# Moving the context queries of three units to earlier places in a fused transformer block

## The chip, the cores and the metric

The kernel runs on one core of one Trainium2 chip. The core has TensorE (PE, matmuls; PEld are its weight loads), VectorE (DVE), ScalarE (ACT), GpSimd (POOL) and SyncE (SP), which here issues nearly all DMAs. The engines run side by side, each through its own list of instructions in a fixed order, and wait for each other on semaphores. The metric is the device time of one execution in microseconds: 1073.81 us is the median of three runs before the change (1072.66 to 1074.61). A profiled execution of the same program took 1075.05 us.

## The reference

One transformer block in fp32, for 2 batches of 1024 tokens of width 256, 16 heads of 64, and a context of 154 tokens of width 192:

```
h = layernorm(x, ln1);  x = attention(h, h,        sa_wq, sa_wk, sa_wv, sa_wo, sa_bo) + x
h = layernorm(x, ln2);  x = attention(h, cond_emb, ca_wq, ca_wk, ca_wv, ca_wo, ca_bo) + x
h = layernorm(x, ln3);  p = h @ ff_w1 + ff_b1;  a, gate = p[..., :DF], p[..., DF:]
out = (a * gelu(gate)) @ ff_w2 + ff_b2 + x

attention: q = xq @ wq; k = xkv @ wk; v = xkv @ wv     (16 heads of 64)
           softmax(q @ k.T / 8) @ v, heads joined, @ wo + bo
```

Everything must be computed for both batches. The self-attention has 1024 keys a head, the context attention 154.

## The kernel before, in words

**Units and slots.** A unit is a batch and a pair of heads: 2 x 8 = 16 units, in the order `units` (unit 0 is batch 0, pair 0; unit 8 is batch 1, pair 0). Self-attention goes through the units in 128 slots `p`, 8 for each unit; slots 120 to 127 belong to unit 15. Context attention follows with 48 slots `c`, 3 for each unit: slot `c` belongs to unit `c // 3`, and `n = c % 3` is its place in it. Then comes the feed-forward stage.

**The order is written out by hand.** All engines' instructions stand in the order in which the two loops record them (`manual_schedule`). There is no planner that reorders them. Each engine works its own list strictly in that order.

**A self-attention slot** (`self_first`, loop at L1324 ff.). TensorE computes scores of 128 rows against 1024 keys in two PSUM tiles (`s`, L526; a tile is two banks, and there are two tiles). VectorE takes the maxima (L712), ScalarE the exponentials (L537) and frees the tile. The halves of a row lie on different partitions, so SP exchanges their maxima and sums by four small DMAs (`exchange`, L547, tile `st`). `join` then works out the factors (GpSimd L555 to L568, ScalarE L561), VectorE takes reciprocals (L640), GpSimd scales the rows (L650), and VectorE transposes them (`turn_group`, L675), one to three slots after their scores. When a half unit's transposes are complete, `self_values` multiplies them by the values (`po`, L578), in two parts, at slots with `p % 4` of 3 and 0. The value products also read a copy of the values with the partition halves exchanged, which `move_values` (L453) makes by DMA in the sixth slot of a unit. The other slots have room for other TensorE work, which `run_work(n, n_side, ...)` takes from three queues: `work` first (projections; each names the number of PSUM banks that it takes, and `n` is reduced by it), then `side` (normalisation of a later stage), then with what is left of `n` `outs` (output projections, `py`, L500).

**The last unit.** `self_beside(15)` puts the context queries of unit 0 (`cross_queries`, `pq_ca`, L369) into `work`, and the values of the context for units 0 and 1 (`context_values`, `pv_ca`, L831) into `held`, which joins `work` at slot 124. Slots 125 and 126 have `n = 1`. Slot 126 also computes the context keys of the last two pairs (`context_keys`, `pk`, L790).

**A projection** of queries: `project_both` (L369) multiplies the normalised, transposed tokens `hT_ln` by one 128-column slice of `ca_wq`, in two PSUM banks, one for each half of the tokens. With `m=KB` the matmuls use 32 columns of the array each, and with `m=HR` 64 columns. ScalarE evacuates both banks (L384) into a tile `q`, from a pool with two buffers for each tag. Queries use the tag `QT`; the self-attention's keys use `KT`.

**PSUM.** `mm_tile` hands out two banks by turns, `sum_tile` two others, and the scores have four. Whoever gets a bank waits until its previous content has been read.

**Slices.** `load_weights` loads a slice of a weight in two DMAs on SP (L134). For `ca_wq` an even pair's slice goes to the buffer `wq`, an odd pair's to `wk`; each tag has one buffer, so a load waits until the queries of two units before have been computed. In context attention the slice of unit `ui + 2` is asked for in the second slot of unit `ui`.

**A context slot** (`cross_first`). Scores for three or two groups of 128 rows (`sc`, L871), maxima (L877), exponentials (L888), reciprocals (L896), scaling on GpSimd (L899), transposes two slots later (`cross_turn`, L915). Once a unit is complete, `cross_regroup` sorts the result by eight DMAs (`wf<-pT_ca`, L932), and `cross_weigh` multiplies by the values (`poc`, L951) in the second slot of a unit, two units later. `cross_values` does this in two parts: the first writes two `sum_tile` banks, the second two `mm_tile` banks. VectorE evacuates `poc` (L965).

**What runs beside the first context slots**: slot 0 the second part of the value products of half 30, slot 1 the queries of unit 1, slot 2 those of unit 2 (in `sum_tile` banks), slots 3 and 4 the value products of the last half, slot 5 two output projections of self-attention (`py_sa`; four are queued there), slot 6 the queries of unit 3 and, in slot 7, a third `py_sa`, the context values of units 2 and 3 (`pv_ca`), the fourth `py_sa` and the first `poc`. From slot 9 on, the first slot of each unit `ui` computes the queries of unit `ui + 1`. In slot 7, ScalarE evacuates `pv_ca` (L841) and VectorE adds `py_sa` to `x` (L507).

**SP's own order** around the end of self-attention: exchange of slot 126, two copies within `held_v` (L843) that belong to `context_values` and are popped from the queue `later`, the slice of unit 2, the exchange of slot 127, four copies of `ends` (L848), the slice of unit 3.

Of the kernel before, what the change touches and what calls it, by code (L numbers as in the profile page):

```python
# [8 lines left out]
F32 = mybir.dt.float32  # L9
# [4 lines left out]
P = 128  # L14
# [4 lines left out]
def tile_transformer_block(ctx: ExitStack, tc: tile.TileContext, a: dict, out: bass.AP):  # L19
# [4 lines left out]
    B, S, D = x.shape  # L24
# [11 lines left out]
    HR = P // 2  # L36
# [3 lines left out]
    KB = 32  # L40
# [20 lines left out]
    p2 = ctx.enter_context(tc.tile_pool(name="p2", bufs=2))  # L61
# [64 lines left out]
    def load_slice(name, c0, n, p):  # L126

        own = w[name][:, c0:c0 + n]
        if p != HR:
            return load_rows(wpool, name[3:], f"{name}_{c0}", own, p)  # L130
        tag = "wk" if name == "ca_wq" and c0 // P % 2 else name[3:]
        t = wpool.tile([P, NH, n], F32, tag=tag, name=f"{name}_{c0}")
        for r0 in range(0, P, HR):
            nc.sync.dma_start(out=t[r0:r0 + HR], in_=own.rearrange("(c p) f -> p c f", p=HR))  # L134
        return t
# [3 lines left out]
    def load_weights(kind, pr, what):  # L139
        if what != "v":  # L140
            wsl[kind, pr, what] = load_slice(f"{kind}_w{what}", pr * P, P, HR)
        elif pr % 2 == 0:
            wsl[kind, pr, what] = load_slice(
                f"{kind}_w{what}", pr * P, VC, HR if kind == "sa" else CC)
# [71 lines left out]
    hT, vs, qk, oT = {}, {}, {}, {}  # L216
# [239 lines left out]
    def costing(n, fn):  # L456

        fn.banks = n
        return fn
# [14 lines left out]
    def self_pieces(b, pr):  # L474


        def q():
            self_unit(b, pr)
            return self_queries(b, pr)

        def k():
            pk = two_banks(f"pk_sa{b}_{pr}")
            project_both(pk, wsl["sa", pr, "k"], hT["sa", b], KB)
            return lambda: take_both(qk["sa", b, pr][1], pk)

        return [costing(2, q), costing(2, k)]
# [104 lines left out]
    def run(piece):  # L591
        done = piece()
        if done is not None:
            (adds if getattr(done, "adds", False) else stores).append(done)
# [32 lines left out]
    units = [(b, pr) for b in range(B) for pr in range(NPAIR)]  # L627
    NU = len(units)
# [94 lines left out]
    held, kept = [], []  # L723

    def self_beside(ui):

        nxt = self_pieces(*units[ui + 1]) if ui + 1 < NU else cross_pieces(*units[0])
        if ui + 1 < NU:
            if ui % 2 == 0 and ui:
                work.append(value_piece(*units[ui], 1))  # L730
            work.extend(nxt)
            if ui == 0:
                work.append(unit_value_piece(*units[1], 0, GT))
            if ui % 2:
                work.append(value_piece(*units[ui + 1], 0))
        else:

            work.extend(nxt[:1])
            held.extend(nxt[1:])
        if ui >= HP:  # L740
            ob, og = divmod((ui - HP) // HP, NQ)
            t0 = (ui % HP) * 2
            out_pieces("sa", ob, og, out_order("sa")[t0:t0 + 2])
        if ui == 1:
            norm_beside("sa", 1)
        if ui in (4, 6):
            add_biases("sa", (ui - 4) // 2)
        if ui == NPAIR + 1:
            norm_beside("ca", 0)

    def load_ahead(p):

        ui, n = divmod(p, 2 * SH)
        for what in "qkv":
            at = {"q": SH - 1 + 2 * (ui == 0), "k": SH + 2, "v": 2 * SH - 1}[what]
            if n != at or ui + 2 >= NU and what == "k":
                continue
            if what == "v" and ui % 2:
                continue
            if ui + 2 < NU:  # L760
                load_weights("sa", units[ui + 2][1], what)
            elif ui + 2 == NU or what == "q":
                load_weights("ca", units[ui + 2 - NU][1], what)
        if p == SA - 2:
            load_weights("ca", units[2][1], "q")
        if p in (LAG + 1, 2 * SH - 1, SA - SH - 6):
            load_keys(2 * (1 + (LAG + 1, 2 * SH - 1, SA - SH - 6).index(p)), 2)

# [2 lines left out]
    CA = len(CG) * NU  # L771
    crossed, pTc = {}, {}

    def cross_queries(b, pr, m=HR, bank=mm_tile):
        q = qk["ca", b, pr] = p2.tile([P, S], F32, tag="QT", name=f"q_ca{b}_{pr}")
        pq = [bank(f"pq_ca{b}_{pr}_{r}") for r in range(2)]
        project_both(pq, wsl["ca", pr, "q"], hT["ca", b], m)
        return lambda: take_both(q, pq, scale)
# [485 lines left out]
    with tc.manual_schedule():  # L1264
# [59 lines left out]
        for p in range(SA):  # L1324
# [21 lines left out]
            ui, n = divmod(p, 2 * SH)  # L1346
# [6 lines left out]
            if hg == LAG:  # L1353
                f = (ui - NPAIR // 2 - 1) * EC
# [4 lines left out]
                if n == SH + LAG and ui in (0, 1, NU - 1):  # L1359

                    pr = {0: 2, 1: 4, NU - 1: 6}[ui]
# [3 lines left out]
        for c in range(CA):  # L1365
# [13 lines left out]
            ui, n = divmod(c, len(CG))  # L1379
            nxt = units[ui + 1] if ui + 1 < NU else None  # L1380
            if n == 0:
                cross_beside(ui)
            elif n == 1 and 1 <= ui < NU - 2:
                load_weights("ca", units[ui + 2][1], "q")
            elif n == 2 and nxt and ui:
                load_weights("ca", nxt[1], "v")
            flush(adds)
# [17 lines left out]
            if c == 0:  # L1405
                run(lambda: self_values(2 * NU - 2, 1))
            elif c == 1:
                run(lambda: cross_queries(*nxt))
            elif c == 2:
                run(lambda: cross_queries(*units[2], bank=sum_tile))  # L1410
            elif c == 3:
                run(lambda: self_values(2 * NU - 1, 0))
            elif c == 4:
                run(lambda: self_values(2 * NU - 1, 1))
            elif n == 0 and ui:
                if nxt:
                    run(lambda: cross_queries(*nxt))
                else:
                    run_work(2, 0)
                run_work(0, 1)  # L1420
            elif n == 1:

                spare["turned"] = True
                run_work(0, 1, sum_tile if outs else None)
                flush(stores)
                run_work(0, 0, n_sum=1)
                if ui % 2 == 0:
                    run(lambda: context_values(*units[ui]))
                run_work(1, 0)
                flush(adds)  # L1430
                flush(slow)
                flush(stores)
                cross_weigh(c)
            elif n == 2:
                run_work(0, ui != HP, sum_tile if ui == HP + 1 else None)
                if c == SH + 1:
                    run_work(2, 0)
                elif ui == HP:
                    wo["ca"] = const.tile([P, NPAIR, D], F32, tag="wo", name="ca_wo")
                    later[1:1] = [lambda i=i: nc.sync.dma_start(  # L1440
                        out=wo["ca"][:, i, :], in_=w["ca_wo"][i * P:(i + 1) * P, :])
                        for i in range(NPAIR)]
# [20 lines left out]
        for k in range(2 * FU):  # L1463
# [18 lines left out]
            while n_left > 0 and sums:  # L1482
                fn, n = sums.pop(0)
# [51 lines left out]
```

## Time and profile before

| | |
|---|---|
| median of three runs | 1073.81 us (1072.66 to 1074.61) |
| profiled execution | 1075.05 us, its span 1073.2 us |
| granted TensorE clock | 1.0 throughout |
| busy: PE, PEld, DVE, ACT, POOL | 1059.4, 716.2, 883.1, 646.9, 777.0 us |
| self-attention, from the start of the span to about | 697.6 us (first context scores `sc`) |
| context attention to about | 897 us (last `sc`) |
| feed-forward | the rest |

A row of a timeline has the start in us from the beginning of the span, the duration in us, the engine, the line, the operation, output and inputs, tile, shape and number of instructions that were merged in this row; in brackets the idle time of the engine before it and what ended it. Matmuls overlap in the pipeline, so a row's duration reaches beyond the next row's start; the time that a group takes is better read from start to start. One fp32 matmul stands as two records. A row of `SPq` is the time that SP spends issuing; the transfer lands later. A line number such as L369 is the line of a helper and shared by all callers, so the tile's name (`pq_ca`, `pq_sa`) tells which.

### The profile page before, as it was taken

Reading aid. Unit: us, or ns where it says so; the run is one execution under the profiler, and the core shown is the slowest. Engines: PE = TensorE matmul, PEld = TensorE weight load, DVE = VectorE, ACT = ScalarE, POOL = GpSimd, SP = SyncE. Lnnn points to the kernel's source line nnn. Section 1 sums busy time; section 2 is a strip of 40 time slices with the busy share of each in tenths; the row PEclk is TensorE's granted clock in tenths of the full one; section 3 lists DMA queues with packets and bytes.
Section 4 is the critical chain, followed back from the end, with each engine's and each line's share of the span. In section 5 each row is a group of like instructions: output and inputs, shape, how many; then the busy total and the mean of one; then the engine's idle time right before and its main releaser. Section 6 shows DMA issues by size and latency. Waiting matters only on the chain.

```text
span 1073.2 us, 48628 instructions
## 1 busy us (share of the span) xinstructions
PE 1059.4 (99%) x20196; PEld 716.2 (67%) x20196; DVE 883.1 (82%) x1321; ACT 646.9 (60%) x2096; POOL 777.0 (72%) x1652
## 2 busy tenths in 40 slices
PE   8999999999999999999999999999999999999998
PEld 6566777556556555555665665466766667788998
DVE  5789899998989989999999899968777887655554
ACT  5766677677666666676777666665566564342231
POOL 2677777778777777677777777776666876499884
PEclk9999999999999999999999999999999999999999
DMA  3132122121021121111111101125776545000000
GB/s 101 38 73 54 29 68 53 25 63 41 22 59 25 34 51 34 39 34 34 44 22 45 44 14 38 36 59 139 164 177 172 123 108 114 16 6 15 21 10 30
DMA packets 86045, 60.95 MB, mean 57 GB/s; under 512 B 32122, under 2 KB 74562, under 8 KB 85826
## 3 DMA queue, kind: packets, MB, share of 16 engines
q1 hardware_dynamic: 84450, 57.07, 22.1%
q8 instruction: 159, 2.61, 1.1%
q10 hardware_dynamic: 1376, 0.79, 0.2%
q14 instruction: 60, 0.49, 0.2%
HBM read 27.91 MB, written 2.10 MB: 28 GB/s over the span
## 4 chain that ended last, share of the span: by engine, by line
PE 74%; DMA 7%; SPq 6%; POOL 6%; DVE 2%; issue 2%; ACT 1%; POOLq 0%; DVEq 0%; ACTq 0%
PE s L526 14%; PE po L578 13%; DMA st<-st 7%; SPq L547 6%; PE py_ca L500 5%; PE py_sa L500 4%; PE poc L951 4%; PE pq_ca L369 4%; PE pq_sa L369 4%; PE pb L1072 4%; PE pk_sa L369 4%; PE pq L1217 3%; PE pv_sa L405 3%; POOL p L650 3%; PE sc L871 2%; PE pa L1072 2%
## 5 line engine op out<-in xcount | busy, mean ns | idle before, releaser
L650 POOL TENSOR_SCALAR p<-p,rd,ee 128x512 f32<-128x512 f32 x512 | 391.9, 771 | 80.0 <-DVE rd L640 79.6
L537 ACT ACTIVATE p<-s,st 128x512 f32<-128x512 f32 x512 | 345.5, 687 | 169.7 <-DVE st L712 164.5
L712 DVE TENSOR_REDUCE st<-s 128x2 f32<-128x1024 f32 x256 | 308.6, 1206 | 56.8 <-issue 17.3
L675 DVE STREAM_TRANSPOSE pT<-p 128x1024 f32<-128x1024 f32 x256 | 302.8, 1219 | 1.5 <-POOL p L650 1.2
L526 PE MATMUL s<-k_sa,q_sa 64*32 64x512 f32 x4096 | 257.8, 591 | 2.8 <-ACT p L537 2.0
L578 PE MATMUL po<-pT,held_v 64*32 64x256 f32 x8192 | 240.8, 376 | 0.7 <-DVE pT L675 0.6
L578 PEld LDWEIGHTS po<-pT,held_v 64*32 64x32 f32 x8192 | 182.5, 106 | 67.0 <-issue 26.0
L526 PEld LDWEIGHTS s<-k_sa,q_sa 64*32 64x32 f32 x4096 | 89.7, 106 | 93.1 <-issue 46.6
L888 ACT ACTIVATE p<-sc,neg 128x154 f32<-128x154 f32 x256 | 96.4, 405 | 78.9 <-DVE rden L896 75.0
L899 POOL TENSOR_SCALAR p<-p,rden 128x154 f32<-128x154 f32 x256 | 97.3, 406 | 51.8 <-DVE rden L896 51.5
L537 ACT ACTIVATION_READ_ACCUMULATOR p<-s,st 128x1 f32 x512 | 104.0, 203 | 0.0
L555 POOL TENSOR_TENSOR dd<-st 128x8 f32<-128x8 f32 x128 | 26.0, 203 | 82.4 <-DMA st<-st 80.6
L500 PE MATMUL py_sa<-sa_wo,o_sa 128*128 128x256 f32 x256 | 59.7, 386 | 1.0 <-ACT held_v L415 1.0
L500 PE MATMUL py_ca<-ca_wo,o_ca 128*128 128x256 f32 x256 | 60.2, 383 | 0.0
L877 DVE TENSOR_REDUCE neg<-sc 128x6 f32<-128x924 f32 (+1 forms) x48 | 47.8, 996 | 14.9 <-PE sc L871 14.9
L369 PE MATMUL pq_ca<-hT_ln,ca_wq 64*64 64x512 f32 (+1 forms) x544 | 59.1, 590 | 0.9 <-DMA ca_wq<-in_L_xattn_ca_wq_dram 0.8
L500 PEld LDWEIGHTS py_sa<-sa_wo,o_sa 128*128 128x128 f32 x256 | 47.3, 190 | 19.0 <-issue 5.2
L369 PE MATMUL pq_sa<-hT_ln,sa_wq 64*32 64x512 f32 (+1 forms) x976 | 57.8, 586 | 0.7 <-ACT held_v L415 0.7
L369 PE MATMUL pk_sa<-hT_ln,sa_wk 64*32 64x512 f32 x960 | 57.1, 590 | 0.2 <-ACT q_sa L384 0.2
L888 ACT ACTIVATION_READ_ACCUMULATOR p<-sc,neg 128x1 f32 x256 | 56.5, 221 | 0.0
L915 DVE STREAM_TRANSPOSE pT_ca<-p 128x480 f32<-128x480 f32 (+1 forms) x96 | 52.9, 587 | 0.9 <-POOL p L899 0.8
L405 PE MATMUL pv_sa<-sa_wv,hT_ln 64*32 64x256 f32 x1792 | 52.9, 376 | 0.0
(158 smaller groups left out, 1476.0 us busy)
## 6 DMA issues: line engine op xcount, KB each, us to landing
wf<-pT_ca SPq DMA_DIRECT2D x128, 128.0 KB, 2.4
st<-st SPq DMA_DIRECT2D x512, 1.0 KB, 2.0
held_v<-held_v SPq DMA_DIRECT2D x32, 256.0 KB, 4.0
sa_wq<-in_L_xattn_sa_wq_dram SPq DMA_DIRECT2D x32, 128.0 KB, 2.8
sa_wk<-in_L_xattn_sa_wk_dram SPq DMA_DIRECT2D x32, 128.0 KB, 3.6
sa_wv<-in_L_xattn_sa_wv_dram SPq DMA_DIRECT2D x16, 256.0 KB, 4.2
ca_wq<-in_L_xattn_ca_wq_dram SPq DMA_DIRECT2D x32, 128.0 KB, 3.1
wf<-in_L_xattn_ff_w_dram SPq DMA_DIRECT2D x12, 256.0 KB
```

What stands on the lines that cost most here:

```text
L369: nc.tensor.matmul(pq[r][f:f + m, at:at + n], lhsT=wt[own, c, f:f + m], rhs=h[own, c, t0:t0 + n], start=(c == 0), stop=(c == NH - 1), tile ...
L405: nc.tensor.matmul(pv[r][f:f + KB, e * VC:(e + 1) * VC], lhsT=h[half, c, t0:t0 + KB], rhs=wt[half, c, :], start=(c == 0), stop=(c == NH - ...
L500: nc.tensor.matmul(py[:, e * D:(e + 1) * D], lhsT=o[:, i, (t + e) * P:(t + e + 1) * P], rhs=wo[kind][:, g * HP + i, :], start=(i == 0), st ...
L526: nc.tensor.matmul(sc[a4 * KB:(a4 + 1) * KB, j, :], lhsT=q[r, c:c + KB], rhs=k[r, h * HB:(h + 1) * HB], start=True, stop=True, tile_positi ...
L537: nc.scalar.activation(pr[:, j, :], sc[:, j, :], AF.Exp, bias=st[:, 0, 0, i, j:j + 1], accum_out=st[:, 0, 1, i, j:j + 1],)
L578: nc.tensor.matmul(po[a2][d:d + KB, :QH // 2], lhsT=v[e][r, t, d:d + KB], rhs=pT[r, d // DH * NK + n, :], start=(t == 0 and e == 0), stop= ...
L650: nc.gpsimd.tensor_scalar(pr[:, j, :], pr[:, j, :], own["rd"][:, c:c + 1], own["ee"][:, 0, c:c + 1], op0=ALU.mult, op1=ALU.mult,)
L675: nc.vector.transpose(halves[h][:, :, c:c + KB], slots[p]["p"][i].rearrange("p j (n k) -> p (j n) k", k=KB))
L712: nc.vector.tensor_reduce(st[:, 0, 0, i, :], sc[i], AX.X, ALU.max, negate=True)
L888: nc.scalar.activation(pr_[:, j, i, :T], sc[:, j, i * T:(i + 1) * T], AF.Exp, bias=neg[:, j, i:i + 1], accum_out=den[:, j, i:i + 1],)
L899: nc.gpsimd.tensor_scalar(pr_[:, j, i, :T], pr_[:, j, i, :T], rden[:, j, i:i + 1], 1.0, op0=ALU.mult, op1=ALU.mult,)
L1072: nc.tensor.matmul(into[:, :BT], lhsT=lhs, rhs=wh[pair][i], start=first, stop=True, skip_group_check=True)
```

## The change

Five edits, one of them the consequence of another:

- The queries of unit 1 leave context slot 1 and join `held`, ahead of the context values. They take two banks, with `m=KB` and the tag `KT`. By the rules of `run_work` they run in slot 125, and the context values, which ran there, in slot 126. The two copies within `held_v` that follow the context values move behind them, into context slot 0, on SP after the exchange of slot 127.
- The queries of units 2 and 3 run in context slots 1 and 2, unit 2 with the tag `QT` in `mm_tile` banks, unit 3 with the tag `KT` in `sum_tile` banks.
- Slot 6 has no queries any more, so it takes two from `outs` (`run_work(2, 0)`): the third and fourth `py_sa` move there from slot 7, and their additions on VectorE to the beginning of slot 7, ahead of its maxima.
- The slice of unit 3 is asked for in slot 126, behind that of unit 2, and so ahead of the exchange of slot 127.
- In context attention the slice of unit `ui + 3`, no longer `ui + 2`, is asked for in the second slot of unit `ui`. It goes into the buffer that the queries of unit `ui + 1`, computed one slot earlier (for unit 2 three slots earlier), have read.

From slot 9 on all engines have the same instructions in the same order as before, but for the slices. TensorE has 16 matmuls more in all, since the queries of unit 1 now use 32 columns each.

```diff
@@ self_beside, for the last unit
             work.extend(nxt[:1])
+            held.append(costing(2, lambda: cross_queries(*units[1], KB, tag="KT")))
             held.extend(nxt[1:])
@@ load_ahead
         if p == SA - 2:
-            load_weights("ca", units[2][1], "q")
+            for u in (2, 3):
+                load_weights("ca", units[u][1], "q")
@@ cross_queries
-    def cross_queries(b, pr, m=HR, bank=mm_tile):
-        q = qk["ca", b, pr] = p2.tile([P, S], F32, tag="QT", name=f"q_ca{b}_{pr}")
+    def cross_queries(b, pr, m=HR, bank=mm_tile, tag="QT"):
+        q = qk["ca", b, pr] = p2.tile([P, S], F32, tag=tag, name=f"q_ca{b}_{pr}")
@@ the loop over context slots
-            elif n == 1 and 1 <= ui < NU - 2:
-                load_weights("ca", units[ui + 2][1], "q")
+            elif n == 1 and 1 <= ui < NU - 3:
+                load_weights("ca", units[ui + 3][1], "q")
...
             elif c == 1:
-                run(lambda: cross_queries(*nxt))
+                run(lambda: cross_queries(*units[2]))
             elif c == 2:
-                run(lambda: cross_queries(*units[2], bank=sum_tile))
+                run(lambda: cross_queries(*units[3], bank=sum_tile, tag="KT"))
...
             elif n == 0 and ui:
-                if nxt:
+                if nxt and ui > 2:
                     run(lambda: cross_queries(*nxt))
                 else:
                     run_work(2, 0)
```

## The prediction

> **What bounds the kernel now.** I read the page first, then the busy time by stretches, then the timelines of TensorE and of the engines and queues that release it. The page:
>
> ```profile
> span 1073.2 us, 48628 instructions
> ## 1 busy us (share of the span) xinstructions
> PE 1059.4 (99%) x20196; PEld 716.2 (67%) x20196; DVE 883.1 (82%) x1321; ACT 646.9 (60%) x2096; POOL 777.0 (72%) x1652
> ```
>
> TensorE has 1073.2 - 1059.4 = 13.8 us without a matmul in the whole span. A change that only reorders work can win little more than what part of these holes it fills. The stretches where the change works (columns: PE, PEld, DVE, ACT, POOL busy):
>
> ```profile
> 680.00:690.00 10.00, 8.74 (x161) 4.25 (x139) 9.94 (x13) 6.76 (x23) 7.40 (x17) 1.00 0.12 29
> 690.00:700.00 10.00, 9.38 (x243) 5.13 (x249) 8.92 (x11) 6.26 (x21) 7.48 (x18) 1.00 0.38 95
> 740.00:750.00 10.00, 9.05 (x142) 5.26 (x138) 9.86 (x27) 7.48 (x36) 9.50 (x28) 1.00 0.61 157
> ```
>
> TensorE lacks 1.26 and 0.62 us in the last self-attention slots (125 to 127) and 0.95 us in the third and fourth unit of context attention; VectorE is nearly full in the first and the third. Their TensorE rows (start, duration, what, idle before it):
>
> ```profile
> 683.85 1.13 PE L831 MATMUL pv_ca<-ca_wv,ctxT 96*128 96x256 f32 x4
> 686.00 1.09 PE L526 MATMUL s<-k_sa,q_sa 64*32 64x512 f32 x16 [1.02 <-ACT p L537]
> 687.33 1.09 PE L526 MATMUL s<-k_sa,q_sa 64*32 64x512 f32 x16 [0.24 <-ACT p L537]
> 688.36 2.42 PE L790 MATMUL pk<-ctxT,ca_wk 96*128 96x320 f32 x8
> 691.09 1.09 PE L526 MATMUL s<-k_sa,q_sa 64*32 64x512 f32 x16 [0.31 <-ACT p L537]
> 692.42 1.09 PE L526 MATMUL s<-k_sa,q_sa 64*32 64x512 f32 x16 [0.24 <-ACT p L537]
> 693.31 4.36 PE L578 MATMUL po<-pT,held_v 64*32 64x256 f32 x128
> ```
>
> Slot 125 has only `pv_ca` beside its scores, and the scores of 126 and 127 wait in four halves (1.02, 0.24, 0.31, 0.24) for a PSUM bank that ScalarE's exponentials hold. That is the room for the moved queries. The softmax tail meets TensorE again at context slot 3:
>
> ```profile
> 711.96 3.69 PE L578 MATMUL po<-pT,held_v 64*32 64x256 f32 x128 [0.61 <-DVE pT L675]
> ```
>
> Here 0.61 us is lost to VectorE's last transposes: up to 0.61 us of lateness of TensorE costs nothing; lateness of the softmax costs in full.
>
> **The change part by part.**
>
> *Queries of unit 1 in slot 125.* Sixteen wide matmuls leave context slot 1; thirty-two narrow ones (32 columns, twice the weight loads) enter. The first unit's queries have that form already:
>
> ```profile
> 662.69 3.64 PE L369 MATMUL pq_ca<-hT_ln,ca_wq 64*32 64x512 f32 x64
> ```
>
> 3.64 us against 3.67 for the wide form (725.31, below): the form costs nothing. Start to start I take 3.43 (725.31 to 728.74). Their slice is asked for only in slot 123:
>
> ```profile
> 680.09 1.39 SPq L134 DMA_DIRECT2D ca_wq<-in_L_xattn_ca_wq_dram  x2
> ```
>
> ```profile
> ca_wq<-in_L_xattn_ca_wq_dram SPq DMA_DIRECT2D x6, 128.0 KB, 3.9
> ```
>
> The second half goes out at about 680.8 and, at 3.9 us to land, is there at 684.7; the queries run to 684.7 + 3.43 = 688.1. Then the scores of 126 (half of 64 such records, 1.72), `pv_ca` now in this slot (0.86, from 731.53 to 732.39 below) and `pk` (2.42): the scores of 127 begin at 693.1 (before 691.09), the value products at 694.8 (before 693.31). But before, these had to wait anyway:
>
> ```profile
> 694.44 2.75 PEld L578 LDWEIGHTS po<-pT,held_v 64*32 64x32 f32 x104 [0.55 <-DMA held_v<-held_v]
> ```
>
> After 24 loads they stood until 694.44 for the moved half of the values, so they ended at 693.31 + 4.36 = 697.7. Now, without that wait, 694.8 + 3.43 and the pipeline's 0.2 give 698.4: 0.7 late, 0.1 more than the 0.61 at slot 3 covers.
>
> *The softmax beside it.* VectorE took the first half of 126 late already:
>
> ```profile
> 688.40 1.15 DVE L712 TENSOR_REDUCE st<-s 128x2 f32<-128x1024 f32 x1
> ```
>
> It will be there at 688.1 + 1.09 = 689.2, 0.8 later. The evacuation of the new queries comes ahead of 126's exponentials on ScalarE, but while these still wait for the maxima: nothing. What counts is the exchange of slot 127 on SP:
>
> ```profile
> 696.74 0.21 ACT L537 ACTIVATION_READ_ACCUMULATOR p<-s,st 128x1 f32 x1
> ```
>
> ```profile
> 695.89 1.23 SPq L843 DMA_DIRECT2D held_v<-held_v  x2
> 697.16 1.35 SPq L134 DMA_DIRECT2D ca_wq<-in_L_xattn_ca_wq_dram  x2
> 698.67 3.20 SPq L547 DMA_DIRECT2D st<-st  x4
> ```
>
> The exponentials of 127 end at 696.95, the exchange leaves at 698.67: the queue came last, with 1.72 to spare. The change swaps the two copies of `held_v` for the two loads of unit 3's slice (1.23 against 1.35, +0.1); that load waits for the queries of slot 125, done at 688.1, so for nothing. The copies follow behind the exchange, some 30 us ahead of their reader (734.21). If 126's exchange, at the head of this queue, slips by its 0.8, so does 127's. Tail in all: between -0.6 (the hole at slot 3 closes, where the transposes come sooner by chance) and +0.9. I take +0.2, because the nearest row, 698.67, stands behind a queue.
>
> The larger load ahead of the exchange is weighed against a rule: the Trainium skill, "DMA: Bandwidth & Descriptors", section "Queues, rings and completion order", says each DMA engine consumes its ring in order, so a small transfer behind a slice waits for it. No row here separates that wait. With the 435 GB/s of the page's section "Specifications" the 128 KB more are an estimated 0.3 us, and the sum would come out 0.3 higher.
>
> *Units 2 and 3 in context slots 1 and 2.* Same form, banks and slots as units 1 and 2 had: 0. Nobody waits for them; their first scores are slots 6 and 9. The second buffer tag is free, as the keys it held were last read in slots 119 and 127.
>
> *Slots 6 and 7.* The stretch before:
>
> ```profile
> 725.31 3.67 PE L369 MATMUL pq_ca<-hT_ln,ca_wq 64*64 64x512 f32 x32
> 728.74 1.03 PE L871 MATMUL sc<-kT,q_ca 64*64 64x154 f32 x24
> 729.70 1.99 PE L500 MATMUL py_sa<-sa_wo,o_sa 128*128 128x256 f32 x8
> 731.53 1.03 PE L831 MATMUL pv_ca<-ca_wv,ctxT 96*128 96x256 f32 x4
> 732.39 1.89 PE L500 MATMUL py_sa<-sa_wo,o_sa 128*128 128x256 f32 x8
> 734.21 1.09 PE L951 MATMUL poc<-wf,held_v 64*64 64x256 f32 x16
> ...
> 736.85 1.49 PE L871 MATMUL sc<-kT,q_ca 64*64 64x154 f32 x40
> ```
>
> The two `py_sa` (1.83 + 1.82 = 3.65) move up into slot 6 in place of the queries (3.43): slot 7's scores start 0.22 late, at 728.96. `pv_ca` follows at 729.9, `poc` could begin at 731.0 and end at 733.6, 3.2 before 736.85. It will not. `poc` has two parts of half its 2.64 us each, and the second writes the two rotating matmul banks. Before, `py_sa` ran between `pv_ca` and `poc` and hid `pv_ca`'s evacuation. Now that cover is gone, and ScalarE does it behind slot 7's exponentials:
>
> ```profile
> 731.07 0.39 ACT L888 ACTIVATE p<-sc,neg 128x154 f32<-128x154 f32 x1 [0.96 <-DVE rden L896]
> ```
>
> ```profile
> 733.27 0.76 ACT L841 COPY held_v<-pv_ca 64x256 f32<-64x256 f32 x2
> ```
>
> ```profile
> 729.83 1.12 DVE L877 TENSOR_REDUCE neg<-sc 128x6 f32<-128x924 f32 x1 [0.89 <-PE sc L871]
> ```
>
> ```profile
> 732.29 0.63 DVE L507 TENSOR_TENSOR x<-py_sa,x 128x512 f32<-128x512 f32 x1
> ```
>
> Worse, the two additions of `py_sa` now stand ahead of slot 7's maximum: the second waits for its matmuls (728.96) and 0.63 more, so the maximum starts near 730.2 instead of 729.83. The copies then end at 733.27 + 0.76 + 0.4 = 734.4; the rest of the second part (1.32 less a sixth, and 0.1 to the release) ends at 735.6. The next scores start 736.85 - 735.6 = 1.2 us sooner, not 3.2. Bounds: 0 and 3.2. From there VectorE is full (9.86 of 10), all its work hangs on that point and moves with it.
>
> *Slices asked sooner.* One hole remains:
>
> ```profile
> 747.95 1.04 PE L369 MATMUL pq_ca<-hT_ln,ca_wq 64*64 64x512 f32 x2
> 749.83 3.23 PE L369 MATMUL pq_ca<-hT_ln,ca_wq 64*64 64x512 f32 x27 [0.85 <-DMA ca_wq<-in_L_xattn_ca_wq_dram]
> ```
>
> ```profile
> 738.16 3.61 PE L369 MATMUL pq_ca<-hT_ln,ca_wq 64*64 64x512 f32 x32
> ```
>
> ```profile
> 744.78 1.38 SPq L134 DMA_DIRECT2D ca_wq<-in_L_xattn_ca_wq_dram  x2
> ```
>
> Two records ran, the other thirty started at 749.83. Unbroken they would have at 747.95 + 2 x 3.43 / 32 = 748.16: 1.67 us lost, the idle column showing half. The new program asks for that slice a unit sooner: the wait goes. The load at 744.78 is then the next unit's, and its buffer's last readers are the queries of the slot before, which ended by 738.16 + 3.61 = 741.77; SP comes to it 3 us later and stands for nothing. Behind the hole come transposes and projections that need VectorE's work of before; I take the whole 1.67 (bounds 0 and 1.67).
>
> *Sum:* +0.2 - 1.2 - 1.67 = -2.7. The profiled execution took 1075.05 us, its span 1073.2 with 1.85 around it, so 1072.4 and a span of 1070.5. It is 1.24 above the median of the three runs, 1073.81; forecast 1073.81 - 2.7 = 1071.1 us. The 0.2% that a measurement can tell from no change is 2.15 us here.
>
> **The rivals.**
>
> *The bank frees in time.* If ScalarE took the copies ahead of the exponentials, slot 7 would give 3.2: 0.2 - 3.2 - 1.67 = -4.7, 1069.1 us. Against it: the program puts them behind.
>
> *VectorE paces (no measurable change).* With VectorE at 9.94 and 9.86 of 10 in two of the three stretches, TensorE's early arrival only turns into waits for it, and closing the slice hole yields nothing: 0.2 - 1.2 = -1.0, 1072.8 us. For it: the first and third row of the stretches. Against it: the wait at 749.83 names the DMA. The Trainium skill, "Perfetto Trace Analysis", section "Identifying the Most-Contended Engine", speaks for it: matmul busy time is no measure for TensorE, weight-load busy time is. The page's 67% against VectorE's 82% agrees with that reading over the span.
>
> *The tail slips.* The exchange of 127 lands over 0.5 us later than assumed, up to the 0.9 and a late landing of the slice: about 1.5 lost instead of 0.2, 1072.4 us.
>
> *The tail is serial (slower).* The queries, the late slice and the evacuation all lie on the chain scores, exponentials, exchange, transposes, value products of slot 3. Price: 0.85 (683.85 to 684.7) + 3.43 + two evacuations at `pv_ca`'s 0.38 or more, 5.1 in all; 5.1 - 2.87 = +2.2, 1076.0 us. It decides from a slip of 5.0 us. Against it: the waits of 1.02, 0.24, 0.31 and 0.24 before the scores, and the 1.72 on SP.
>
> **How the numbers follow.** Forecast 0.52, bank free 0.08, VectorE 0.16, tail slips 0.14, serial 0.10. A tenth of the forecast's own share ends inside the 0.2% (its range is 1070.0 to 1072.2). Faster: 0.47 + 0.08 + 0.03 from slips that still clear it = 0.58; same 0.31, the rest of these and of VectorE; slower 0.11. The range reaches from 1069.0, the free bank, to 1074.2, where the serial tail is only half paid.
>
> **What the new profile would show.** Scores of 126 and 127 without idle before them; the hole at context slot 3 between 0 and 1.5; a hole inside slot 7's `poc`, released by ScalarE's copy of `pv_ca`, 1.5 to 2.5 us long; no DMA wait in the sixth unit's queries. I am wrong if the exchange of 127 leaves SP well after 699.5, or if TensorE idles for VectorE after 750.

## The result, and the profile after

The changed kernel took 1069.97 us (median of 7 runs, 1069.1 to 1071.75) beside 1074.24 us of the kernel before (7 runs): a ratio of 0.9963, 95% interval 0.9953 to 0.9973, so 2.9 to 5.0 us faster. Two later comparisons gave 0.9973 (0.9962 to 0.9985) and 0.9975 (0.9965 to 0.9984). The forecast, 2.7 us less, lies just outside the first interval, whose medians differ by 4.3 us, and inside the other two. The profiled execution took 1071.75 us, its span 1069.1 at a granted clock of 1.0. The page, with the chain that ended last by engine:

```profile
span 1069.1 us, 48669 instructions
...
PE 1057.3 (99%) x20228; PEld 709.8 (66%) x20228; DVE 882.9 (83%) x1321; ACT 645.3 (60%) x2096; POOL 774.8 (72%) x1652
...
PE 92%; DVE 2%; DMA 2%; POOL 2%; SPq 1%; ACT 1%; issue 1%; DVEq 0%; POOLq 0%
```

TensorE's idle time went from 13.8 to 1069.1 - 1057.3 = 11.8 us. The stretches of the prediction, and the one of slot 7 (columns: PE, PEld, DVE, ACT, POOL busy):

```profile
680.00:690.00 10.00, 9.47 (x165) 4.13 (x150) 8.36 (x11) 5.98 (x18) 6.58 (x15) 1.00 0.13 30
690.00:700.00 10.00, 10.00 (x256) 6.36 (x262) 9.19 (x11) 7.05 (x25) 6.80 (x16) 1.00 0.41 107
730.00:740.00 10.00, 8.62 (x136) 6.11 (x138) 8.55 (x22) 5.62 (x28) 6.47 (x19) 1.00 0.47 100
740.00:750.00 10.00, 10.00 (x167) 6.12 (x159) 9.86 (x29) 7.35 (x37) 9.31 (x25) 1.00 0.62 153
```

The stretch of slots 126 and 127 (second row) and the one with the sixth unit's queries (last row) are full now. Two holes are left in these rows: 0.53 us at 683 and 1.38 us near 732. TensorE's rows of slots 125 to 127 and of context slot 3 (start, duration, what, idle before it):

```profile
683.01 3.70 PE L369 MATMUL pq_ca<-hT_ln,ca_wq 64*32 64x512 f32 x57 [0.53 <-DMA ca_wq<-in_L_xattn_ca_wq_dram]
...
688.79 1.13 PE L833 MATMUL pv_ca<-ca_wv,ctxT 96*128 96x256 f32 x4
689.75 2.32 PE L792 MATMUL pk<-ctxT,ca_wk 96*128 96x320 f32 x8
692.00 1.95 PE L526 MATMUL s<-k_sa,q_sa 64*32 64x512 f32 x32
693.74 3.66 PE L578 MATMUL po<-pT,held_v 64*32 64x256 f32 x128
...
711.26 3.69 PE L578 MATMUL po<-pT,held_v 64*32 64x256 f32 x128
```

The four waits for a bank are gone, the value products no longer stop for the moved half of the values, and at context slot 3 (711.26) TensorE has no idle time: it arrives last there, not VectorE's transposes. Slots 7 and the sixth unit:

```profile
731.28 0.61 PE L953 MATMUL poc<-pT_ca,held_v 64*64 64x256 f32 x8
731.72 0.60 PE L953 MATMUL poc<-wf,held_v 64*64 64x256 f32 x4
733.69 0.86 PE L953 MATMUL poc<-wf,held_v 64*64 64x256 f32 x10 [1.38 <-ACT held_v L843]
...
744.85 1.02 PE L873 MATMUL sc<-kT,q_ca 64*64 64x154 f32 x24
745.69 3.61 PE L369 MATMUL pq_ca<-hT_ln,ca_wq 64*64 64x512 f32 x32
749.12 0.96 PE L873 MATMUL sc<-kT,q_ca 64*64 64x154 f32 x24
```

```profile
730.68 0.39 ACT L890 ACTIVATE p<-sc,neg 128x154 f32<-128x154 f32 x1 [2.27 <-DVE rden L898]
...
732.88 0.76 ACT L843 COPY held_v<-pv_ca 64x256 f32<-64x256 f32 x2
```

The second part of `poc` issued four records, and 1.97 us passed from the first of them to the next one (731.72 to 733.69). It stood until ScalarE's second copy of `pv_ca`, behind slot 7's exponentials, freed the bank. The sixth unit's queries run unbroken, 3.43 from start to next start.

**A common measure.** For every profile below, the table has the times from the start of VectorE's maxima of one slot to those of another, as the difference from the first profile of the kernel before (there 33.40, 21.08, 24.90 and 134.86 us): "tail" from self-attention slot 125 to context slot 4, "slot 7" from 4 to 8, "unit 6" from 8 to 14, "later" from 14 to 47. "At 125" is where slot 125's maxima start, against 683.25. Minus is sooner.

| profile | at 125 | tail | slot 7 | unit 6 | later | sum from 125 |
|---|---|---|---|---|---|---|
| after | -1.44 | +0.73 | -1.26 | -2.22 | +0.07 | -2.68 |
| control_before | -2.63 | +0.18 | 0 | -0.68 | +0.91 | +0.41 |
| after_again | -0.96 | +0.33 | -1.26 | -2.20 | +0.10 | -3.03 |
| after_third | -1.54 | +0.31 | -1.25 | -2.22 | +0.10 | -3.06 |
| slices_only | +1.31 | +0.14 | 0 | -2.24 | +0.10 | -2.00 |
| slices_again | +0.72 | -0.50 | 0 | -2.24 | +0.20 | -2.54 |
| moves_only | -0.30 | +0.22 | -1.25 | +0.01 | +0.88 | -0.14 |
| q1_alone | -2.38 | -1.05 | 0 | -0.78 | +2.97 | +1.14 |
| slice1_early | -0.31 | -0.72 | -1.26 | -2.25 | +0.09 | -4.14 |
| slice3_late | -1.39 | +0.23 | -1.26 | -2.22 | +0.09 | -3.16 |
| pv_early | +0.95 | +0.26 | -0.66 | -2.24 | +0.10 | -2.54 |
| split_cover | -1.14 | +0.41 | -1.98 | -2.20 | +0.09 | -3.68 |
| split_slice1 | -1.65 | -0.49 | -1.98 | -0.65 | +0.05 | -3.07 |

Four profiles have the tail of the kernel before unchanged (before, control_before, slices_only, slices_again), and theirs runs from -0.50 to +0.18: a smaller difference between two single tails shows nothing. "Slot 7", and "unit 6" with the sooner slices, repeat within 0.05.

### The profile page after: what moved, and what is told of

The parts are those of the page before. It is cut to its first block, busy times and chain, and to the rows that moved or that the text cites. A ratio compares the mean times of both kernels' runs of the same rounds, so it can differ in the third digit from the quotient of the medians.

```text
span 1069.1 us, 48669 instructions
## 1 busy us (share of the span) xinstructions
PE 1057.3 (99%) x20228; PEld 709.8 (66%) x20228; DVE 882.9 (83%) x1321; ACT 645.3 (60%) x2096; POOL 774.8 (72%) x1652
## 4 chain that ended last, share of the span: by engine, by line
PE 92%; DVE 2%; DMA 2%; POOL 2%; SPq 1%; ACT 1%; issue 1%; DVEq 0%; POOLq 0%
PE po L578 20%; PE s L526 20%; PE py_ca L500 5%; PE py_sa L500 5%; PE pk_sa L369 5%; PE pq_sa L369 5%; PE pq_ca L369 5%; PE pv_sa L405 4%; PE poc L953 4%; PE pb L1074 4%; PE pq L1219 4%; PE sc L873 3%; PE pa L1074 2%; PE pc L1074 2%; PE pf L1249 1%; PE ph_ln L286 1%
## 5 line engine op out<-in xcount | busy, mean ns | idle before, releaser
L578 PEld LDWEIGHTS po<-pT,held_v 64*32 64x32 f32 x8192 | 177.3, 106 | 72.5 <-issue 25.2
L879 DVE TENSOR_REDUCE neg<-sc 128x6 f32<-128x924 f32 (+1 forms) x48 | 47.8, 996 | 12.0 <-PE sc L873 11.8
```

The lines of the kernel that those rows point to most:

```text
L578: nc.tensor.matmul(po[a2][d:d + KB, :QH // 2], lhsT=v[e][r, t, d:d + KB], rhs=pT[r, d // DH * NK + n, :], start=(t == 0 and e == 0), stop= ...
```

## Experiments

Ratios are to the kernel before on the same chip, with 95% intervals; medians of 7 to 12 runs.

**The two kernels again, unchanged** (control_before, after_again).

> The kernel before, unchanged, against itself: a ratio of 1.000, and a median within 0.1% of the other one's. What it is for: in the two profiles at hand 1.44 us of the 4.11 us between the ends arose in self-attention's slots 112 to 116, ahead of the first moved instruction, where both programs are the same. If that is chance from execution to execution (theory A), the maxima of this kernel's slots will lie up to 1.5 us away from those of the first profile somewhere ahead of slot 125, and from there on keep a constant distance. If it comes from the change, through the places of instructions and buffers in memory (theory B), this profile lies within 0.3 us of the first one at slot 125.

> The changed kernel, unchanged. Theory A (only the moved work counts): from slot 125 on it gains 2.7 us on the kernel before (tail +0.7, slot 7 -1.3, slices -2.1), so 0.25% and a ratio of 0.9975. Theory B (the new program is also faster ahead of its change): the start of slot 125 comes 1 us or more sooner than in the kernel before and the ratio stays at 0.9963 or below.

control_before: 1.0001 (0.9987 to 1.0015). after_again: 0.9973 (0.9962 to 0.9985). The queries of the first unit, slots ahead of the change, start at 662.69 in the first profile of before and in these at (the kernel before, then the changed kernel first and again):

```profile
660.07 3.64 PE L369 MATMUL pq_ca<-hT_ln,ca_wq 64*32 64x512 f32 x64
```

```profile
661.26 3.64 PE L369 MATMUL pq_ca<-hT_ln,ca_wq 64*32 64x512 f32 x64
```

```profile
661.73 3.64 PE L369 MATMUL pq_ca<-hT_ln,ca_wq 64*32 64x512 f32 x64
```

The same program was 2.62 us sooner there in another execution, so the 1.44 us that after's profile had won ahead of the change lie within what executions of one program differ by (theory A). Only what comes from slot 125 on is the change's: -2.68, -3.03 and -3.06 in its three profiles. But theory A had also expected that the kernel before keeps a constant distance from slot 125 on, and that is false: control_before won 0.68 in the sixth unit and lost 0.91 later.

**The slices alone** (slices_only; slices_again is the same kernel). The kernel before with:

```diff
-            elif n == 1 and 1 <= ui < NU - 2:
-                load_weights("ca", units[ui + 2][1], "q")
+            elif n == 1 and 1 <= ui < NU - 3:
+                for u in range(3 if ui == 1 else ui + 3, ui + 4):
+                    load_weights("ca", units[u][1], "q")
```

> The kernel before, with the query slices of the fourth unit and later asked for one unit sooner and nothing moved on TensorE. Prediction's theory: the wait in the sixth unit's queries (1.67 us by the start of its 3rd to 32nd record) goes and nothing takes its place: -1.7 us, ratio 0.9984. If the profile of after is read right, -2.1 us, 0.9980. Rival (VectorE paces that stretch): the time that TensorE wins turns into waits for VectorE within a unit, -0.3 to 0, ratio 0.9997 to 1.000.

> The kernel before with the sooner slices alone, once more. If its first result (0.9971) holds, the sooner slices are worth 3 us, more than the one wait of 1.67 us that the profile of before shows; by the traces of the four kernels with the late slices (waits of 2.2, 2.4, 3.1 and 4.5 us in all, at other units in each execution) the expected worth is 3.1 us, ratio 0.997. If the prediction's 1.67 is right, 0.9984.

0.9971 (0.9957 to 0.9984) and, beside other runs, 0.9972 (0.9959 to 0.9984): about 3 us each, more than the prediction's 1.67 or the 2.2 us of the trace, at least by the middle of the interval. All the queries of context attention in the groups of TensorE's instructions from 680 to 900 us, slices_only:

```profile
L369 PE MATMUL pq_ca<-hT_ln,ca_wq 64*64 64x512 f32 x480 | 54.5, 589 | 0.0
```

No wait is left, nor do the queries wait from context slot 1 on in any other profile with the sooner slices. There each slice of the fifth unit and later is asked for at least 14 us ahead of its first reader. What is won in the sixth unit stays won: "later" is within 0.2 us of zero there. It does not turn into waits of TensorE for VectorE. The rival falls.

**The moves alone** (moves_only). The changed kernel with:

```diff
-            elif n == 1 and 1 <= ui < NU - 3:
-                load_weights("ca", units[ui + 3][1], "q")
+            elif n == 1 and 2 <= ui < NU - 2:
+                load_weights("ca", units[ui + 2][1], "q")
```

> The changed kernel, but from the fourth context unit on the slices are asked for when they were before. Prediction's theory: the tail (+0.2, by the profile of after +0.7) and slot 7 (-1.2) remain, and the wait for the sixth unit's slice returns, longer by what TensorE arrives sooner, unless SP asks sooner as well: between -1.0 and +0.2, 0.9991 to 1.0002. Rival (VectorE paces): the slices are worth nothing, so all of after's gain is here, -2.7, ratio 0.9975.

1.0006 (0.9992 to 1.002). Tail and slot 7 are there, -1.03 together; the wait in the sixth unit is there in full, and a second one came at 824 us, where the first profile of before has none:

```profile
747.52 4.22 PE L369 MATMUL pq_ca<-hT_ln,ca_wq 64*64 64x512 f32 x29 [1.00 <-DMA ca_wq<-in_L_xattn_ca_wq_dram]
...
824.43 4.03 PE L369 MATMUL pq_ca<-hT_ln,ca_wq 64*64 64x512 f32 x30 [0.23 <-DVE neg L879]
```

The second row names VectorE ahead of it, but is itself broken inside: 4.03 us for 30 records where 32 take 3.61; in q1_alone below the same queries name the DMA. Without the sooner slices the time shows no gain from the moves. The unchanged kernel waits at more than one place too. In control_before:

```profile
745.80 4.14 PE L369 MATMUL pq_ca<-hT_ln,ca_wq 64*64 64x512 f32 x29 [0.40 <-DMA ca_wq<-in_L_xattn_ca_wq_dram]
...
797.61 3.96 PE L369 MATMUL pq_ca<-hT_ln,ca_wq 64*64 64x512 f32 x29
```

The second group shows no idle time ahead of it, yet takes 3.96 us for 29 records, and its slot (24) is 0.89 us longer than in slices_only.

**Unit 1's queries alone** (q1_alone). The kernel before with the first edit of the change; unit 2's queries stay in context slot 2, and slot 1 has none (the new argument `tag` is left out here):

```diff
+            held.append(costing(2, lambda: cross_queries(*units[1], KB, tag="KT")))
...
             elif c == 1:
-                run(lambda: cross_queries(*nxt))
+                pass
```

> The kernel before, with only the second unit's queries moved into slot 125; context slot 1 has nothing in their place. 3.43 us of TensorE's work leave the stretch ahead of context slot 3. Theory (the softmax of slots 126 and 127 sets the arrival at slot 3): TensorE comes to the value products of slot 3 early and waits there for VectorE's transposes, about 3 us; from there on the program is the one of before, and the time is that of before plus the tail's slip: 0 to +0.7 us, ratio 1.0000 to 1.0007. Rival (TensorE alone sets the pace there, the chain of softmax has room): nearly all of the 3.4 us that left context slot 1 is won, against 0.9 to 1.3 us of holes filled in slots 125 to 127: -1 to -3 us, ratio 0.9972 to 0.9990.

0.9994 (0.9977 to 1.0011). The expectation's premise was wrong: the 3.43 us do not leave the stretch ahead of context slot 3, they only go from slot 1 to slot 125. So the tail can only win what holes the queries fill. In this one profile it won 1.05 us; the rest waits for the transposes, 1.76 us in place of 0.61:

```profile
708.52 3.69 PE L578 MATMUL po<-pT,held_v 64*32 64x256 f32 x128 [1.76 <-DVE pT L675]
```

This checks the tail of the whole change: -1.05 + 3.43 (the queries of unit 3, which the change adds ahead of slot 3) - 1.76 (the hole that they fill) = +0.62, measured +0.73, +0.33 and +0.31. In this profile what followed took the gain back: it waited for slices in three units,

```profile
744.79 4.06 PE L369 MATMUL pq_ca<-hT_ln,ca_wq 64*64 64x512 f32 x29 [0.44 <-DMA ca_wq<-in_L_xattn_ca_wq_dram]
...
796.89 1.04 PE L369 MATMUL pq_ca<-hT_ln,ca_wq 64*64 64x512 f32 x2 [0.31 <-DVE rden L897]
798.14 3.23 PE L369 MATMUL pq_ca<-hT_ln,ca_wq 64*64 64x512 f32 x27 [0.21 <-DMA ca_wq<-in_L_xattn_ca_wq_dram]
...
823.67 4.01 PE L369 MATMUL pq_ca<-hT_ln,ca_wq 64*64 64x512 f32 x30 [0.58 <-DMA ca_wq<-in_L_xattn_ca_wq_dram]
```

and "later" is +2.97. The time, with an interval from -2.5 to +1.2 us, shows neither. SP asked for the slice of the second of them at 792.13, with its first reader at 796.89:

```profile
792.13 1.37 SPq L134 DMA_DIRECT2D ca_wq<-in_L_xattn_ca_wq_dram  x2
```

From 700 to 900 us the slices of this execution took 2.8 to 6.0 us to land, median 3.5:

```profile
DMA to landing us min/median/max: 2.8/3.5/6.0
```

So with the late slices it depends on the landing whether a unit waits. The sixth unit's slice is asked for only 3.2 to 3.5 us ahead of its first reader (744.78 to 747.95 in the first profile), and its slots lost 1.5 to 2.2 us in all four profiles with the late slices. The slices of the eighth, tenth and every second later unit are asked for 4.3 to 6.4 us ahead, and their slots lost 0.9 to 1.8 us in some executions: slot 24 in control_before and q1_alone, slot 30 in moves_only and q1_alone. Against the profiles with the sooner slices (unit 6 and later together -2.1), the four with the late ones lost 2.1 (before), 2.4 (control_before), 3.0 (moves_only) and 4.3 us (q1_alone), 2.95 in the mean. The two kernels with the slices alone were about 3 us faster by their times, which agrees.

**Unit 1's slice sooner** (slice1_early). The changed kernel with:

```diff
-            elif ui + 2 == NU or what == "q":
+            elif ui + 2 == NU:
                 load_weights("ca", units[ui + 2 - NU][1], what)
+        if p == SA - 2 * SH:
+            load_weights("ca", units[1][1], "q")
```

> The changed kernel, with the second unit's slice asked for at slot 112 and no longer at slot 123. Theory: the wait of 0.53 us for it inside slot 125's queries goes, and as TensorE is late, not the softmax, at context slot 3 (no idle there in the profile of after), the whole comes 0.5 us sooner, up to 0.7 with what TensorE then still has to wait for: 0.05%, ratio 0.0005 below the changed kernel's. Rival (the softmax sets the arrival at slot 3): no change, and an idle time of about 0.5 us for the transposes returns at slot 3.

0.9966 (0.995 to 0.9982). The expectation names slot 112, but `SA - 2 * SH` is slot 120, and SP issued the slice at 663.36, 20 us ahead of its reader. The wait is gone:

```profile
683.40 3.64 PE L369 MATMUL pq_ca<-hT_ln,ca_wq 64*32 64x512 f32 x64
```

From the start of slot 125's scores to `pv_ca`, 7.00 us pass here and in split_slice1 below, and 7.96 to 8.23 us in the eight profiles with the late slice. So the wait cost 1.0 to 1.2 us, at least twice what the idle column shows (0.53 in after, 0.28 to 0.44 in four others, nothing in three): as in the sixth unit, it shows the wait ahead of the first row only. The tail is -0.72 in place of +0.31 to +0.73, and -0.49 in split_slice1. At slot 3 no idle time came back, so in the changed kernel TensorE was late there, not the softmax. In split_slice1 a short one did come back, so with the sooner slice the two arrive nearly together:

```profile
709.82 3.69 PE L578 MATMUL po<-pT,held_v 64*32 64x256 f32 x128 [0.16 <-DVE pT L675]
```

The time does not separate this kernel from the changed one.

**Unit 3's slice behind the exchange** (slice3_late). The changed kernel with:

```diff
-        if p == SA - 2:
-            for u in (2, 3):
-                load_weights("ca", units[u][1], "q")
+        if p in (SA - 2, SA - 1):
+            load_weights("ca", units[p - SA + 4][1], "q")
```

> The changed kernel, with the fourth unit's slice asked for a slot later, behind the maxima's exchange of slot 127 and not ahead of it. Theory (TensorE sets the arrival at context slot 3): the exchange leaves SP about 1.3 us sooner, its transposes end sooner, and the time stays: within 0.3 us of the changed kernel, an idle of zero at slot 3 either way. Rival (the queue of the exchange is what the tail lost): 0.5 to 0.7 us less than the changed kernel.

0.9979 (0.9964 to 0.9993). The exchange of slot 127 left SP at 697.15, 5.11 us behind the one of 126; in after_again, 5.65 behind. First slice3_late, then after_again:

```profile
692.04 2.44 SPq L547 DMA_DIRECT2D st<-st  x4
694.53 1.99 SPq L134 DMA_DIRECT2D ca_wq<-in_L_xattn_ca_wq_dram  x2
697.15 3.49 SPq L547 DMA_DIRECT2D st<-st  x4
```

```profile
692.57 2.44 SPq L547 DMA_DIRECT2D st<-st  x4
695.06 3.00 SPq L134 DMA_DIRECT2D ca_wq<-in_L_xattn_ca_wq_dram  x4
698.22 3.11 SPq L547 DMA_DIRECT2D st<-st  x4
```

That is 0.54 sooner, not the expected 1.3 (two issues fewer took 1.0 less), and the tail is +0.23 against +0.33 and +0.31: no change that one profile can show, as the theory said. Nothing speaks for the queue of the exchange as what the tail lost.

**The third unit's values ahead of both projections** (pv_early). The changed kernel with `context_values(*units[2])` run in context slot 6 ahead of `run_work(2, 0)`, and not in slot 7:

```diff
+                    if nxt and ui == 2:
+                        run(lambda: context_values(*units[2]))
                     run_work(2, 0)
...
-                if ui % 2 == 0:
+                if ui % 2 == 0 and ui > 2:
```

> The changed kernel, with the third unit's context values computed in context slot 6, ahead of the two output projections that stand there, and no longer between the scores of slot 7 and its value products. Theory (the hole of 1.97 us inside slot 7's value products is a bank waiting for ScalarE's copy, which stands behind slot 7's exponentials): the copy is done under the projections, the hole goes, and up to 2.0 us more are won than by the change: ratio to the kernel before 0.9945 (2.7 + 2.0 = 4.7 us less, plus what is won ahead of the change if that is no chance). Rival (VectorE paces from there): the hole only moves to a wait for VectorE in slots 8 to 10, less than 0.5 us more than the change, 0.997.

0.9976 (0.9962 to 0.9991). Slot 7 gave -0.66, worse than the change's -1.26. The wait moved to the second projection, which rotates through the same two banks; the copy that frees its bank stands behind slot 6's exponentials. A second wait for ScalarE came, at the scores of slot 9:

```profile
727.60 1.89 PE L500 MATMUL py_sa<-sa_wo,o_sa 128*128 128x256 f32 x8
731.01 1.99 PE L500 MATMUL py_sa<-sa_wo,o_sa 128*128 128x256 f32 x8 [1.52 <-ACT held_v L843]
...
737.64 1.02 PE L873 MATMUL sc<-kT,q_ca 64*64 64x154 f32 x24 [0.57 <-ACT p L890]
```

The theory's cause is confirmed (the same copy ends the wait), its remedy is not; the rival is wrong in its cause, VectorE, for both waits name ScalarE. It is right in that the hole only moves.

**One projection back between the values and their use** (split_cover, and with unit 1's slice sooner split_slice1). The changed kernel with:

```diff
-                    run_work(2, 0)
+                    run_work(1 if nxt else 2, 0)
...
-                run_work(0, 0, n_sum=1)
+                run_work(0, 0, n_sum=0 if ui == 2 else 1)
```

> The changed kernel, with one of the two output projections of context slot 6 put back into slot 7, between the third unit's values and the value products. Theory (the hole of 1.97 us in slot 7 is a bank waiting for a copy that stands on ScalarE behind slot 7's exponentials): the scores of slot 7 come 1.8 us sooner, and with them the exponentials and the copy; the projection's 1.8 us lie over the wait, and 0 to 0.5 us of the hole are left: 1.5 to 2.0 us less than the changed kernel from slot 8 on. Rival (as the value product moved ahead of both projections did: the wait only moves): the hole stands then in front of the projection, and less than 0.5 us is won.

> The same, and the second unit's slice asked for at slot 112. If both holes are independent, their gains add: in the trace 1.5 to 2.0 us in slot 7 and 1.1 to 1.4 us between slots 125 and 127 (what slice1_early won there against the two profiles of the changed kernel), 2.6 to 3.4 us less than the changed kernel, ratio to the kernel before 0.994 to 0.995. If one only hands its time to the next wait for VectorE, no more than the better one of the two alone, 0.996.

split_cover: 0.9976 (0.9964 to 0.9987). Slot 7 gave -1.98, 0.7 better than the change; 1.5 to 2.0 had been expected. The time does not show it.

```profile
727.56 1.13 PE L833 MATMUL pv_ca<-ca_wv,ctxT 96*128 96x256 f32 x4
728.84 1.99 PE L500 MATMUL py_sa<-sa_wo,o_sa 128*128 128x256 f32 x8 [0.15 <-DVE x L507]
...
732.11 0.60 PE L953 MATMUL poc<-wf,held_v 64*64 64x256 f32 x4
732.94 0.86 PE L953 MATMUL poc<-wf,held_v 64*64 64x256 f32 x10 [0.24 <-ACT held_v L843]
```

The projection now waits for the addition that frees its bank (`pv_ca` to it 1.28 us, 0.86 in the kernel before), and 0.83 us still pass from the four records of `poc` to the next. split_slice1: 0.9974 (0.9964 to 0.9984). It reached slot 8 with tail and slot 7 at -2.47, against -0.93 in after_again, so there the gains add, to 1.5 us and not to the expected 2.6 to 3.4; in slot 10 it gave 1.48 back, not to VectorE but to a transfer:

```profile
741.72 0.86 PE L955 MATMUL poc<-wf,held_v 64*64 64x256 f32 x10 [1.44 <-DMA wf<-pT_ca]
```

SP issues eight transfers of the regrouped softmax one behind the other, behind two copies of the values. In split_cover, then split_slice1:

```profile
732.52 1.16 SPq L845 DMA_DIRECT2D held_v<-held_v  x2
733.79 5.42 SPq L934 DMA_DIRECT2D wf<-pT_ca  x8
```

```profile
731.12 2.06 SPq L847 DMA_DIRECT2D held_v<-held_v  x2
733.27 5.31 SPq L936 DMA_DIRECT2D wf<-pT_ca  x8
```

TensorE came to slot 9's queries 1.41 us sooner (734.19 against 735.60), the transfers only 0.52, which is no more than the profile's lead at slot 125, as the copies ahead of them took 0.9 longer. Whether SP would be late in every execution one profile can't tell.

**The changed kernel beside the slices alone** (after_third, on the chip of slices_again).

> The changed kernel once more, beside the next one, to tell what the moved queries are worth once the slices are asked for sooner. By the traces (tail +0.3 to +0.7, slot 7 -1.25): 0.5 to 0.9 us less than the kernel with the sooner slices alone. By the times so far (median 1072.43 against 1072.04): nothing, or a loss of up to 0.5.

0.9975 (0.9965 to 0.9984), 1071.03 us against 1071.64 us of slices_again, 0.9972 (0.9959 to 0.9984). The first pair had 0.9973 against 0.9971. In the traces the moves are worth 0.65 us (the mean of -2.68, -3.03 and -3.06 against that of -2.00 and -2.54); the times can't separate that from nothing. No kernel tried is shown to be faster than the changed one.

## Why the prediction was right, and where it was not

- **Queries of unit 1 in slot 125.** Shown: they ran where they were put, without a wait before the scores of 126 and 127. They started at 683.01, which is 684.45 on the clock of the first profile (1.44 later), against 684.7 predicted, and did not run unbroken; the scores of 127 started at 692.00, there 693.44, against 693.1. Right within 0.4 us.
- **The tail, +0.2.** Measured +0.73, +0.33 and +0.31, inside the bounds; the seven profiles with this tail, unit 1's slice late, run from +0.22 to +0.73. The size of this term was too small. The prediction had TensorE 0.7 late and 0.6 of it covered at slot 3, and the rest of the +0.2 from the exchange's queue. TensorE was 1.0 to 1.2 late at the first context scores (697.33 in after, 698.77 on the first profile's clock, against 697.60), as much as the late slice cost (slice1_early). The softmax did not slip: the last transposes ended 28.0 to 28.8 us after the start of slot 125's maxima in these seven profiles, and 28.1 to 28.7 in the four with the tail of before. The exchange left SP at 698.54, 699.98 on the first profile's clock, and so a little behind the announced 699.5, without harm. For the Trainium skill's rule ("DMA: Bandwidth & Descriptors", "Queues, rings and completion order") this means: a slice fewer ahead of the exchange (slice3_late) changed the time by nothing measurable here, so no run shows its estimated 0.3 us.
- **Slot 7, -1.2.** Measured -1.26, -1.26, -1.25. Cause, place and size were right: `poc`'s second part stood still until the second copy of `pv_ca`, which pv_early and split_cover confirmed. The 3.2 us of the rival "the bank frees in time" were never there.
- **Slices, -1.67.** The mechanism was right, the term too small in two ways. In the profile itself the lost time was 2.2. The prediction counted from the queries' first record at 747.95, which was late itself. TensorE's row ahead of it, in the kernel before:

```profile
746.83 1.02 PE L871 MATMUL sc<-kT,q_ca 64*64 64x154 f32 x24
```

  Unbroken, the queries follow these scores after 0.84 us (744.85 to 745.69 in the changed kernel), so at 747.67: 0.28 more. The remaining 0.27 were lost after the group went on at 749.83, for a reason left open. And the prediction took "one hole remains" from one execution: the three others with late slices waited in the sixth unit too, and elsewhere as well, 2.95 us in the mean of the four. (The stretch from 740 to 750 us, which the prediction puts in the third and fourth unit, holds slots of the fourth and fifth.) The slices alone explain nearly all of the measured gain.
- **VectorE paces.** Wrong, and shown so by slices_only: 2.24 us won in a stretch where VectorE is 9.86 of 10 busy arrive at the end undiminished. The Trainium skill ("Perfetto Trace Analysis", "Identifying the Most-Contended Engine") holds matmul busy time for no good measure of TensorE and asks for weight-load busy time, beside the share of peak FLOPs. By weight loads it spoke for this rival: 67% against VectorE's 82%, and 66% against 83% after the change. Here the waits told the bound, not these shares. The chain that ended last is mostly TensorE too, but its share differs between executions, from 74% in the first profile of the kernel before to 92% in after, so a single share proves little.
- **The tail slips, the tail is serial.** Neither: no tail came near the 1.5 us of the first rival or the 5.1 us of the second (its 2.2 is the sum left after the gains elsewhere).
- **The sum, -2.7.** The traces gave -2.7, -3.0 and -3.1 from slot 125 on, the ratios -4.0, -2.9 and -2.7. That the sum came out near is in part luck: the errors of two terms (tail 0.1 to 0.5 short, slices 0.5 or more short) stood against each other. Of the 4.1 us between the first two profiles, 1.44 arose ahead of the change.

## What to carry to other kernels

A hole in one profile is one draw: where loads are asked for 3 to 6 us ahead of their readers and land after 2.8 to 6.0, their expected cost is that over all such loads and executions, not the one wait that happens to be visible. Compare profiles from the last point where both programs are the same, not from the start. Work moved off a spot may have been the cover for an evacuation; before filling a hole, ask which bank the next matmuls rotate into and behind what on ScalarE its release stands.

## What the runs showed of the hardware that was not expected

The same instructions reached slot 125 between 2.63 us sooner and 1.31 us later than in the first profile, at a granted clock of 1.0 in each. The differences arise in steps at single places in self-attention: between slots 112 and 116 the first profile took 0.74 us more than each of the others. What makes them was not looked into. The idle column of a merged row understates a wait on a load that comes in two halves: 0.85 us shown, 2.2 lost; 0.53 shown, 1.2 lost.
